# Cross-attention with layer norm on one core: small products, centring and one store moved in the last four tiles

## Chip, cores and metric

The kernel runs on one core of a Trainium2 chip. The metric is the device time in microseconds (us); lower is better. In the text PE is TensorE (matrix products), DVE is VectorE, ACT is ScalarE, POOL is GpSimd, and SP is SyncE, which in this kernel issues every transfer between HBM and the on-chip memory.

## The reference

There are 16 batches of 256 query rows of width 256, and 77 keys of width 192 for each batch. Eight heads of width 256 attend, and a layer norm over each row of 256 ends the computation:

```python
Q = (img_embed @ Wq).reshape(B, -1, H, D).transpose(0, 2, 1, 3)
K = (sent_embed @ Wk).reshape(B, -1, H, D).transpose(0, 2, 1, 3)
V = (sent_embed @ Wv).reshape(B, -1, H, D).transpose(0, 2, 1, 3)
score = jnp.einsum('bhqd,bhkd->bhqk', Q, K) / math.sqrt(D)
score = jnp.where(mask, score, -jnp.inf)
attn = jax.nn.softmax(score, axis=-1)
ctx = jnp.einsum('bhqk,bhkd->bqhd', attn, V).reshape(B, -1, H * D)
out = ctx @ Wo + img_embed
mu = jnp.mean(out, axis=-1, keepdims=True)
var = jnp.var(out, axis=-1, keepdims=True)
return (out - mu) * jax.lax.rsqrt(var + EPS) * gamma + beta
```

All data are float32. Only the last line and the sum before it concern the change.

## The kernel before

The 4096 query rows are cut into 32 tiles of 128 rows, two to a batch. A tile's rows lie on the 128 partitions; its slice of `xg` (128x256) first holds the input rows, then the sum with the attention's result, then the normalised rows, in place. Eight tiles form a group with one `xg` buffer. After a set-up stage that folds the weights together, a loop runs over the batches as a pipeline: the scores of batch b+1, the weighted sum of batch b and the layer norm of batch b-1 are issued in one turn. The order in which each engine receives its instructions is the order of the program text, written out by hand; nothing reorders it. An engine works through its own queue in that order and waits on semaphores for the others.

The last tile is number 31 (`last`). After the loop the tiles 28 to 31 are still to be finished. Each goes through these steps, whose names and lines the profile shows:

- `attend(t)`, L378: TensorE makes the attention's result `po`.
- `finish(t)`: VectorE adds `po` to the tile (L476) and takes the row statistics (L484, L487) into `mv`, the mean and the variance of each row. Tiles 28 and 29 have had this in the last turn of the loop.
- `spread(first, last)`, L495: ScalarE takes the square root of variance plus epsilon, giving `std`.
- `invert(first, last, aside)`: VectorE takes the reciprocal `rstd` (L502). For the tiles in `aside`, GpSimd then makes `less` = -mean times `rstd`, one number for each row (L506): the "small product".
- `normalise(t, aside)`. For a tile that is set aside, ScalarE computes tile times `rstd` plus `less` (L520), and GpSimd multiplies by gamma (L521) and adds beta (L522). For another tile VectorE does it in two passes: (tile - mean) times gamma (L524, which we call the centring), then times `rstd` plus beta (L527).

Tiles 29 and 30 are set aside; 28 and 31 are VectorE's. The stores go out on SP's queue: tiles 28 and 29 by one transfer of 256 KB (L535) as soon as both are done, 30 and 31 each by its own of 128 KB (L529), issued inside `normalise`. When the tail begins, GpSimd is still busy with the passes of tiles 26 and 27. The tail reads:

```python
    invert(last - 3, last - 1, aside=(last - 2,))
    normalise(last - 2, aside=True)
    finish(last - 1)
    spread(last - 1, last)
    normalise(last - 3)
    invert(last - 1, last, aside=(last - 1,))
    normalise(last - 1, aside=True)
    finish(last)
    spread(last, NT)
    invert(last, NT)
    normalise(last)
```

Of the kernel before, what the change touches and what calls it, by code (L numbers as in the profile page):

```python
# [11 lines left out]
ALU = mybir.AluOpType  # L12
# [41 lines left out]
def kernel(  # L54
# [13 lines left out]
    nc = tc.nc  # L68
# [5 lines left out]
    NG = B // GB  # L74
    QT = S // P
    NT = B * QT
    GT = GB * QT
# [50 lines left out]
    gam = const.tile([P, DI], F32, tag="gam", name="gam")  # L128
    bet = const.tile([P, DI], F32, tag="bet", name="bet")
    xg_of = {}  # L130

    x_rows = x.rearrange("b (t p) d -> p (b t) d", p=P)
    out_rows = out.rearrange("b (t p) d -> p (b t) d", p=P)
# [23 lines left out]
    xT_of, a_of, vw_of, p_of, mv_of = {}, {}, {}, {}, {}  # L157
# [215 lines left out]
    def attend(t):  # L373
        b, pT = t // QT, pT_of.pop(t)
        po = ps_mm.tile([P, DI], F32, tag="mm", name=f"po_{t}")
        for n in range(NF + 1):
            for i in range(NM):
                nc.tensor.matmul(  # L378
                    po[i * BK : (i + 1) * BK],
                    pT[:, n, i],  # L380
                    vw_of[b][:, 2 - n // 2 * 2 : 4 - n // 2 * 2, n % 2, :] if n < NF else vr[:, b, :],
                    start=(n == 0),
                    stop=(n == NF),
                )
        po_of[t] = po
# [92 lines left out]
    def finish(t):  # L478
        if t in po_of:
            add_product(t)  # L480
        g, j = t // GT, t % GT
        y = xg_of[g][:, j, :]
        bn = st.tile([P, 6], F32, tag="bn", name=f"bn_{t}")
        nc.vector.bn_stats(bn, y)  # L484
        if j == 0:
            mv_of[g] = st.tile([P, GT, 2], F32, tag="mv", name=f"mv_{g}", bufs=2)
        nc.vector.bn_aggr(mv_of[g][:, j, :], bn)  # L487
# [3 lines left out]
    def spread(first, last):  # L491

        g, lo, hi = first // GT, first % GT, (last - 1) % GT + 1
        std = st.tile([P, GT], F32, tag="std", name=f"std_{first}")
        nc.scalar.activation(std[:, lo:hi], mv_of[g][:, lo:hi, 1], AF.Sqrt, bias=eps)  # L495
        std_of[first, last] = std

    def invert(first, last, aside=()):

        g, lo, hi = first // GT, first % GT, (last - 1) % GT + 1  # L500
        rstd = st.tile([P, GT], F32, tag="rstd", name=f"rstd_{first}")
        nc.vector.reciprocal(rstd[:, lo:hi], std_of.pop((first, last))[:, lo:hi])  # L502
        if aside:
            less = st.tile([P, GT], F32, tag="less", name=f"less_{first}")
            for j in (t % GT for t in aside):
                nc.gpsimd.tensor_scalar(  # L506
                    less[:, j : j + 1], mv_of[g][:, j, 0:1], rstd[:, j : j + 1], -1.0,
                    ALU.mult, ALU.mult,
                )
        for t in range(first, last):  # L510
            j = slice(t % GT, t % GT + 1)
            rstd_of[t] = rstd[:, j], less[:, j] if aside else None

    def normalise(t, aside=False):

        g, j = t // GT, t % GT
        rstd, less = rstd_of.pop(t)
        y = xg_of[g][:, j, :]
        if aside:
            nc.scalar.activation(y, y, AF.Identity, bias=less, scale=rstd)  # L520
            nc.gpsimd.tensor_tensor(y, y, gam, ALU.mult)  # L521
            nc.gpsimd.tensor_tensor(y, y, bet, ALU.add)  # L522
        else:
            nc.vector.scalar_tensor_tensor(  # L524
                y, y, mv_of[g][:, j, 0:1], gam, ALU.subtract, ALU.mult
            )
            nc.vector.scalar_tensor_tensor(y, y, rstd, bet, ALU.mult, ALU.add)  # L527
        if t >= NT - QT:
            nc.sync.dma_start(out_rows[:, t, :], y)  # L529
            return  # L530
        done.append(t)
        if t ^ 1 in done:
            t |= 1
            j |= 1
            nc.sync.dma_start(  # L535
                out_rows[:, t + 1 - QT : t + 1, :], xg_of[g][:, j + 1 - QT : j + 1, :]
            )
# [4 lines left out]
    with tc.tile_pool(name="wonce", bufs=1) as wp:  # L542
# [23 lines left out]
        first = -(-GB * S2 // CR)  # L566
# [261 lines left out]
    last = NT - 1  # L828
    for b in range(-1, B - 1):
# [9 lines left out]
        g, n = (b + 1) // GB + 1, (b + 1) % GB  # L839
# [22 lines left out]
        if b < NS:  # L862
            if now:
                seven(b)
            nc.scalar.activation(warm, eps, AF.Exp)
            if old:
                invert(old[0], old[-1] + 1)
                normalise(old[0])
            for t in new:
                turn(t)  # L870
            if n >= NF - 2:
                for j in range((n - NF + 2) * GT // 2, (n - NF + 3) * GT // 2, 2):
                    transpose_x(g, j)
            if old:
                normalise(old[1])
            if now:
                add_seven(b)
            if b + 1 < NS:
                sums(b + 1)
            continue  # L880
        for t in now:
            attend(t)
        if b < B - 2:
            invert(old[0], old[-1] + 1, aside=old[:1])
            normalise(old[0], aside=True)
            nc.scalar.activation(warm, eps, AF.Exp)
            turn(new[0])
            normalise(old[1])
            turn(new[1])
            for t in now:  # L890
                add_product(t)
        else:
            turn(new[0])
            invert(old[0], old[-1] + 1, aside=old)
            for t in old:
                normalise(t, aside=True)
            turn(new[1])
            for t in now:
                finish(t)
            spread(now[0], now[-1] + 1)  # L900


    for t in new:
        attend(t)
    invert(last - 3, last - 1, aside=(last - 2,))
    normalise(last - 2, aside=True)
    finish(last - 1)
    spread(last - 1, last)
    normalise(last - 3)
    invert(last - 1, last, aside=(last - 1,))  # L910
    normalise(last - 1, aside=True)
    finish(last)
    spread(last, NT)
    invert(last, NT)
    normalise(last)


# [29 lines left out]
```

## Time and profile before

| what | value |
|---|---|
| median of three runs | 282.15 us (280.95, 282.15, 282.51) |
| the profiled execution, whole time | 280.93 us |
| its span (first to last instruction) | 279.2 us |
| granted TensorE clock | 0.993 |
| busy: PE, DVE, ACT, POOL | 269.7, 206.0, 166.4, 168.2 us |
| start of the last closing instructions (L942) | 278.0 to 279.1 us |
| store of 128 KB, issue to landing | 1.7 us |
| store of 256 KB, issue to landing | 2.3 us |

The span lies inside the whole time; 1.73 us lie around it. In a timeline each line gives the start in us from the span's beginning, the duration, the engine, the line of the kernel, the operation, the written and read tiles with their shapes, and in brackets how long the engine had been idle and which instruction released it. SPq is SP's queue of transfers: the time there is that of the issue, not of the transfer. The waits list adds up such idle times by engine and line.

### The profile page before, as it was taken

What the parts mean: (1) busy time and instruction counts of PE and PEld (TensorE: products, weight loads), DVE (VectorE), ACT (ScalarE), POOL (GpSimd) and SP (SyncE); (2) the same over time, 40 slices, a digit from 0 to 9 for tenths busy, and PEclk for the clock granted to TensorE, in tenths of its full rate; (3) what the DMA queues carried; (4) which work ended last, traced back from release to release, by engine and by line L of the source; (5) the groups of instructions that cost most, each with busy time, mean ns of one, the idle gap of its engine ahead of it and who ended that gap; (6) DMA issues with size and microseconds to landing.
All of it is one profiled execution on the core that took longest, in us unless ns stands there. A gap on an engine that the chain in (4) does not pass through costs nothing.

```text
span 279.2 us, 13274 instructions
## 1 busy us (share of the span) xinstructions
PE 269.7 (97%) x5924; PEld 194.8 (70%) x5924; DVE 206.0 (74%) x421; ACT 166.4 (60%) x447; POOL 168.2 (60%) x228
## 2 busy tenths in 40 slices
PE   8899999999999999999999999999999999999990
PEld 7756599976495959595959585858686858476550
DVE  0353953777738989878788888787787878788873
ACT  2303222146738586868676767777776766978751
POOL 1000069947677777787877777777778445426183
PEclk9999999999999999999999999999999999999997
DMA  6997999920000101940100009501001011010112
GB/s 198 247 223 154 305 262 236 225 82 4 2 6 2 40 5 41 190 155 4 42 2 30 16 25 190 172 5 42 4 5 40 2 42 38 4 41 2 40 39 77
DMA packets 35641, 22.61 MB, mean 81 GB/s; under 512 B 17712, under 2 KB 34048, under 8 KB 35584
## 3 DMA queue, kind: packets, MB, share of 16 engines
q1 hardware_dynamic: 35584, 21.77, 31.1%
q8 instruction: 46, 0.75, 1.2%
q14 instruction: 11, 0.09, 0.1%
HBM read 17.57 MB, written 4.19 MB: 78 GB/s over the span
## 4 chain that ended last, share of the span: by engine, by line
PE 88%; DMA 3%; POOL 2%; ACT 2%; DVE 1%; SPq 1%; issue 0%; ACTq 0%; POOLq 0%
PE ps L313 23%; PE pa L199 12%; PE pv L241 9%; PE po L429 9%; PE pm L429 7%; PE pa L213 6%; PE pv L252 5%; PE po L378 5%; DMA c_sb<-in_ctx_dram 3%; PE pu L676 3%; PE pr L274 2%; ACT e L342 1%; PE pw L690 1%; PE pgb L676 1%; PE pr L284 1%; PE pc L653 1%
## 5 line engine op out<-in xcount | busy, mean ns | idle before, releaser
L342 ACT ACTIVATE e<-s,top 128x77 f32<-128x77 f32 x256 | 67.1, 346 | 52.1 <-DVE top L335 49.9
L356 POOL TENSOR_TENSOR p<-e,rden 128x512 f32<-128x512 f32 x64 | 45.9, 739 | 46.7 <-DVE rden L350 46.4
L313 PE MATMUL ps<-a,xT 128*32 128x154 f32 x2048 | 70.0, 294 | 0.0
L313 PEld LDWEIGHTS ps<-a,xT 128*32 128x32 f32 x2048 | 66.1, 110 | 1.7 <-issue 0.8
L328 DVE TENSOR_TENSOR s<-ps,bias 128x308 f32<-128x308 f32 x64 | 30.3, 474 | 17.7 <-PE ps L313 15.9
L199 PE MATMUL pa<-cA,gA 128*32 128x308 f32 x512 | 35.8, 423 | 0.0
L462 POOL TENSOR_TENSOR xg<-xg,m 128x256 f32<-128x256 f32 x33 | 24.2, 732 | 13.5 <-DVE xg L476 11.8
L199 PEld LDWEIGHTS pa<-cA,gA 128*32 128x32 f32 x512 | 16.4, 110 | 20.9 <-issue 8.0
L241 PE MATMUL pv<-uA,cA 128*32 128x512 f32 x256 | 30.4, 592 | 0.0
L366 DVE STREAM_TRANSPOSE pT<-p 128x640 f32<-128x640 f32 x32 | 25.6, 824 | 2.4 <-POOL p L356 2.4
L348 DVE TENSOR_REDUCE den<-e 128x8 f32<-128x616 f32 x32 | 24.7, 772 | 3.4 <-ACT e L342 3.4
L335 DVE TENSOR_REDUCE top<-s 128x8 f32<-128x616 f32 x32 | 25.5, 795 | 1.1
L664 POOL COPY cB<-cB 64x224 f32<-64x224 f32 (+1 forms) x6 | 1.9, 359 | 35.2 <-DVE cB L153 35.2
L392 POOL TENSOR_TENSOR ts<-vw 128x768 f32<-128x768 f32 x11 | 21.9, 1995 | 0.0
L213 PE MATMUL pa<-cB,gB 64*32 64x308 f32 x512 | 19.5, 420 | 0.0
L378 PE MATMUL po<-vw,pT 128*32 128x256 f32 x320 | 19.2, 380 | 0.0
L859 ACT COPY vw<-pv 128x512 f32<-128x512 f32 x32 | 16.9, 579 | 2.5 <-PE pv L252 2.5
L495 ACT ACT_TABLE_LOAD x14 | 18.0, 1283 | 0.3
L213 PEld LDWEIGHTS pa<-cB,gB 64*32 64x32 f32 x512 | 9.7, 107 | 11.3 <-issue 7.6
L252 PE MATMUL pv<-uB,cB 64*32 64x512 f32 x256 | 17.4, 601 | 0.0
L524 DVE SCALAR_TENSOR_TENSOR xg<-xg,mv,gam 128x256 f32<-128x256 f32 x25 | 17.1, 683 | 0.0
L378 PEld LDWEIGHTS po<-vw,pT 128*32 128x32 f32 x320 | 10.0, 110 | 9.5 <-DVE den L348 2.5
(114 smaller groups left out, 444.9 us busy)
## 6 DMA issues: line engine op xcount, KB each, us to landing
xT<-in_x_dram SPq DMA_DIRECT2D x16, 256.0 KB, 6.2
xg<-in_x_dram SPq DMA_DIRECT2D x4, 1024.0 KB, 7.9
out_dram<-xg SPq DMA_DIRECT2D x15, 256.0 KB, 2.3
wo<-in_L_xattn_Wo_dram SPq DMA_DIRECT2D x4, 512.0 KB, 6.2
wvT<-in_L_xattn_Wv_dram SPq DMA_DIRECT2D x16, 96.0 KB, 3.0
wq_nat<-in_L_xattn_Wq_dram SPq DMA_DIRECT2D x2, 512.0 KB, 5.9
wq_blk<-in_L_xattn_Wq_dram SPq DMA_DIRECT2D x8, 128.0 KB, 5.1
wk_blk<-in_L_xattn_Wk_dram SPq DMA_DIRECT2D x8, 96.0 KB, 5.6
```

Source lines behind the costliest of these rows:

```text
L199: nc.tensor.matmul(flat(o[i * BK : (i + 1) * BK]), gA[:, h, cols(dc, i)], flat(cA[:, batches, :]), start=not B_first, stop=B_first,)
L213: nc.tensor.matmul(flat(banks[j + k][i * BK : (i + 1) * BK]), gB[half(k), h % NF, cols(dc, i)], flat(cB[half(k), batches, :]), start=B_fir ...
L241: nc.tensor.matmul(pv[k][i * BK : (i + 1) * BK], cA[:, b, k * BK : (k + 1) * BK], uA[:, parts, :, i], start=True, stop=False,)
L252: nc.tensor.matmul(pv[k][i * BK : (i + 1) * BK], cB[half(k), b, k * BK : (k + 1) * BK], uB[half(k), parts, :, i], start=False, stop=True,)
L313: nc.tensor.matmul(ps[m // 2][i * BK : (i + 1) * BK, m % 2 * 2 * S2 : (m % 2 + 1) * 2 * S2], xT_of[g][:, j * NM + m, dc], flat(a_of[g][:, ...
L328: nc.vector.tensor_tensor(s[:, a * H // 2 : (a + 1) * H // 2], ps[a][:, : H // 2 * S2].rearrange("p (h k) -> p h k", k=S2), bias[:, b, :]. ...
L335: nc.vector.tensor_reduce(top, s, AX.X, ALU.max, negate=True)
L342: nc.scalar.activation(e[:, h], s[:, h], AF.Exp, bias=top[:, h : h + 1])
L356: nc.gpsimd.tensor_tensor(part, e_mh[:, :, :, keys], rden_mh.unsqueeze(3).to_broadcast(list(part.shape)), ALU.mult,)
L366: nc.vector.transpose(pT_of[t].rearrange("p n m q -> p m n q"), p.rearrange("p m (n k) -> p m n k", k=BK),)
L378: nc.tensor.matmul(po[i * BK : (i + 1) * BK], pT[:, n, i], vw_of[b][:, 2 - n // 2 * 2 : 4 - n // 2 * 2, n % 2, :] if n < NF else vr[:, b, ...
L429: nc.tensor.matmul(out[i * BK : (i + 1) * BK], weight[:, i], moving, start=(n == 0), stop=(n == len(terms) - 1),)
```

## The change

In the tail, VectorE instead of GpSimd makes the small products of tiles 29 and 30. The first of VectorE's two passes becomes a function of its own, `centre`; for tile 28 it is issued ahead of the reciprocal of tiles 28 and 29, and for tile 31 ahead of the reciprocal of tile 31. The stores of tiles 30 and 31 leave `normalise` and are issued at the very end of the program text: that of 30 by ScalarE, behind the root of 31, and that of 31 by SP. The other uses of `invert` and `normalise` keep their instructions.

```diff
-    def invert(first, last, aside=()):
+    def invert(first, last, aside=(), less_on=nc.gpsimd):
...
-                nc.gpsimd.tensor_scalar(
+                less_on.tensor_scalar(
                     less[:, j : j + 1], mv_of[g][:, j, 0:1], rstd[:, j : j + 1], -1.0,
                     ALU.mult, ALU.mult,
                 )
...
+    def centre(t):
+        y = xg_of[t // GT][:, t % GT, :]
+        nc.vector.scalar_tensor_tensor(
+            y, y, mv_of[t // GT][:, t % GT, 0:1], gam, ALU.subtract, ALU.mult
+        )
+
+    def normalise(t, aside=False, centred=False):
...
-            nc.vector.scalar_tensor_tensor(
-                y, y, mv_of[g][:, j, 0:1], gam, ALU.subtract, ALU.mult
-            )
+            if not centred:
+                centre(t)
             nc.vector.scalar_tensor_tensor(y, y, rstd, bet, ALU.mult, ALU.add)
         if t >= NT - QT:
-            nc.sync.dma_start(out_rows[:, t, :], y)
             return
...
     for t in new:
         attend(t)
-    invert(last - 3, last - 1, aside=(last - 2,))
+    centre(last - 3)
+    invert(last - 3, last - 1, aside=(last - 2,), less_on=nc.vector)
     normalise(last - 2, aside=True)
     finish(last - 1)
     spread(last - 1, last)
-    normalise(last - 3)
-    invert(last - 1, last, aside=(last - 1,))
+    normalise(last - 3, centred=True)
+    invert(last - 1, last, aside=(last - 1,), less_on=nc.vector)
     normalise(last - 1, aside=True)
     finish(last)
     spread(last, NT)
+    centre(last)
     invert(last, NT)
-    normalise(last)
+    normalise(last, centred=True)
+    for t, queue in ((last - 1, nc.scalar), (last, nc.sync)):
+        queue.dma_start(out_rows[:, t, :], xg_of[NG - 1][:, t % GT, :])
```

More of the change, by code (lines that the diff above doesn't have):

```diff
@@ L512, in invert @@
             rstd_of[t] = rstd[:, j], less[:, j] if aside else None
-    def normalise(t, aside=False):
+    def centre(t):
[4 more added lines that the diff above has]
+    def normalise(t, aside=False, centred=False):
         g, j = t // GT, t % GT
```

## The prediction

> **What bounds the kernel now.** I read the page first: engine shares, then the chain that ended last.
>
> ```profile
> PE 269.7 (97%) x5924; PEld 194.8 (70%) x5924; DVE 206.0 (74%) x421; ACT 166.4 (60%) x447; POOL 168.2 (60%) x228
> ```
>
> TensorE carries 88% of the chain, but its last matmul (attend of tile 31) starts at 269.57 and the group ends at 271.91. All that the diff touches lies after 269.4 us, in the 9.8 us up to the span's end at 279.2. So I read the timeline of that tail, engine by engine.
>
> ```profile
> 269.25 0.18 DVE L487 BATCH_NORM_AGGREGATE mv<-bn 128x2 f32<-128x6 f32 x1
> ...
> 269.79 0.17 DVE L502 RECIPROCAL rstd<-std 128x2 f32<-128x2 f32 x1 [0.36 <-ACT std L495]
> 269.85 0.73 POOL L522 TENSOR_TENSOR xg<-xg,bet 128x256 f32<-128x256 f32 x1
> ...
> 270.56 0.27 POOL L506 TENSOR_SCALAR less<-mv,rstd 128x1 f32<-128x1 f32 x1
> ...
> 270.86 0.60 ACT L520 ACTIVATE xg<-xg,less,rstd 128x256 f32<-128x256 f32 x1 [1.10 <-POOL less L506]
> 270.88 0.45 DVE L524 SCALAR_TENSOR_TENSOR xg<-xg,mv,gam 128x256 f32<-128x256 f32 x1
> ...
> 271.36 0.49 DVE L527 SCALAR_TENSOR_TENSOR xg<-xg,rstd,bet 128x256 f32<-128x256 f32 x1
> ...
> 271.54 0.89 POOL L521 TENSOR_TENSOR xg<-xg,gam 128x256 f32<-128x256 f32 x1 [0.72 <-ACT xg L520]
> 271.77 0.16 DVE L502 RECIPROCAL rstd<-std 128x1 f32<-128x1 f32 x1
> ...
> 273.21 0.26 POOL L506 TENSOR_SCALAR less<-mv,rstd 128x1 f32<-128x1 f32 x1
> 273.51 0.60 ACT L520 ACTIVATE xg<-xg,less,rstd 128x256 f32<-128x256 f32 x1 [1.86 <-POOL less L506]
> 274.01 0.28 ACT L495 ACTIVATE std<-mv,eps 128x1 f32<-128x1 f32 x1
> 274.19 0.72 POOL L521 TENSOR_TENSOR xg<-xg,gam 128x256 f32<-128x256 f32 x1 [0.72 <-ACT xg L520]
> 274.33 0.16 DVE L502 RECIPROCAL rstd<-std 128x1 f32<-128x1 f32 x1 [1.25 <-ACT std L495]
> 274.41 0.79 DVE L524 SCALAR_TENSOR_TENSOR xg<-xg,mv,gam 128x256 f32<-128x256 f32 x1
> 274.99 0.78 POOL L522 TENSOR_TENSOR xg<-xg,bet 128x256 f32<-128x256 f32 x1
> 275.23 0.83 DVE L527 SCALAR_TENSOR_TENSOR xg<-xg,rstd,bet 128x256 f32<-128x256 f32 x1
> 275.80 0.83 SPq L529 DMA_DIRECT2D out_dram<-xg  x2
> ```
>
> Three things are to be seen. First, the bound of the tail is GpSimd's order. The reciprocal of tile 30 is ready at 271.93, but its small product waits in GpSimd's queue behind the two passes of tile 29 until 273.21: 1.3 us. ScalarE idles 1.86 us for it, and the root of tile 31, whose statistics end at 273.08, stands behind it until 274.01; VectorE idles 1.25 us for that root. Second, VectorE's two passes over tile 31 take 0.79 and 0.83 beside GpSimd, against 0.45 and 0.49 over tile 28. They end at 275.20 and 276.06, each 0.28 after the GpSimd pass beside it (274.91, 275.77). Third, the last store is issued at about 276.26 (two issues of 0.35 to 0.38 each from 275.80), though its data were ready at 276.06. The waiting at the end is the closing line of the program:
>
> ```profile
> L942 SPq EVENT_SEMAPHORE  x8: 17/28/28, 278.0 to 279.1; - x8
> ```
>
> Landing takes 1.75 us (278.0), closing another 1.2.
>
> **What the Trainium skill says.** "SBUF — State Buffer", Who interferes with whom: a VectorE operation with two SBUF inputs and a GpSimd operation that reads SBUF exclude each other for the whole instruction. The trace agrees: the ends 0.28 after GpSimd's are VectorE's bare run after a lock, and the pass at 271.54 took 0.89 instead of 0.73 when it met L527. "DMA: Bandwidth & Descriptors", Issuing engines are not separate DMA queues: issuing from a second engine saves only the sequencer's issue time. Here that is about 0.2 us, and no store of this trace was issued by ScalarE. The same SBUF section says that a VectorE tensor_scalar may enter a mode that takes the shared port too; no VectorE tensor_scalar of this size is in the trace, so it stays open below.
>
> **The change, part by part.** I write the tail out again with the same durations, lock included.
>
> *Centre of 28, ahead of the reciprocal of 28/29.* Its cover is the idle 0.36 before 269.79. It asks at 269.45, meets GpSimd's L521 until 269.77 and ends at 270.05 (+0.28), so the reciprocal slips from 269.79 to 270.07: +0.28. Behind it stand the small product, ScalarE's pass of 29 and all of tile 30. GpSimd's L522 of 27 grows by 0.05, which nothing waits for.
>
> *Small product of 29 on VectorE.* No row has it; bounds are 0.16 (reciprocal 128x1) and 0.18 (aggregate) free of the lock, or an end at GpSimd's 270.63 if it locks. I take 0.17: 270.28 to 270.45. ScalarE's pass of 29 starts at 270.49 instead of 270.86, ends at 271.09; GpSimd's passes run 271.16 to 271.89 and 271.97 to 272.75 (before 273.23).
>
> *Tile 30.* Sum and statistics (0.40 + 0.43 + 0.18 with gaps: 1.08) run 270.47 to 271.55, against 270.96 before: later by 0.6, since VectorE did more ahead of them. Root: 271.58 to 271.86. Second pass of 28 meets L521 and ends at 271.89 + 0.28 = 272.17. Reciprocal to 272.26, small product to 272.47. ScalarE's pass: 272.50 to 273.10, **1.01 earlier** than 273.51. GpSimd: 273.17 to 273.90 and 273.98 to 274.76 (before 275.77). GpSimd's two small products (0.27 + 0.26) leave its queue; the wait at 273.21 goes.
>
> *Tile 31.* The sum, ready to run at 271.98 before, now waits for VectorE until 272.47: +0.5. Statistics end at 273.57 (before 273.08), root 273.60 to 273.88, since ScalarE is free at 273.10. Centre meets L521 and ends at 273.90 + 0.28 = 274.18; the root is inside it. Reciprocal to about 274.30, last pass waits for L522 to 274.76 and ends at 275.04. Before: 276.06. **1.02 earlier.** What is late next is GpSimd's second pass of tile 30.
>
> *Stores.* Issue of 30 goes from SP to ScalarE at 274.80; behind it ScalarE has nothing. It is put behind the root of 31, so it holds up no work. SP issues 31 at 275.08 instead of 276.26: 1.18 earlier. SP keeps only the store of 28/29 before it (GpSimd's 272.75, issue 0.37, gone by 273.2). The two transfers' data took about 0.4 each in windows of 0.1 us before (276.65 to 277.1, 277.15 to 277.6), so they overlap by 0.1 at most: price 0 to 0.1. ScalarE's first use of its queue: bounded below by 0, above by the first load of SP's queue, 2.8 us to landing for 256 KB against 2.1 for stores of that size, 0.7 extra; store 30 has 0.28 in hand (274.80 + 1.75 = 276.55 against 276.83), so 0.4 shows at most. I take 0.
>
> Sum: 1.18 less 0.03 for the overlap, **1.15 us**. Span 279.2 to 278.05, the profiled execution 280.93 to 279.8. The median of the runs shown is 282.15, 1.22 above that execution; on it the sum gives 281.0, a gain of 0.41%. A measurement of this kernel tells about 0.5% (1.41 us) from no change, so the likeliest verdict is no change with a gain behind it.
>
> **The rivals.**
> 1. *The small product takes the lock.* Then each of the two ends at the end of a GpSimd pass: 29's at 270.70 (+0.25), 30's behind the L522 of 29, near 273.06 (+0.6 in all). For it: the skill's sentence. Against: one element per partition offers nothing to split. End of VectorE 275.64, last issue 275.68, gain 0.6: 281.55. Chance 0.2.
> 2. *VectorE wins its races for the port*, or the issue and closing shrink as well. If neither pass of tile 31 waits, tile 31 ends at about 274.65 and store 30 at 274.80 decides: gain up to 1.45, 280.7, just over the bound. Against: GpSimd's pass is under way at each request. Chance 0.15.
> 3. *A second queue costs more than it saves*: slower. Its place is store 30 and the ends of the program; its price, at most 0.4 shown by first use, the closing (1.2) and the 1.73 outside the span each taken twice: 3.3 in all, net 2.2 slower, 284.3. It eats the gain at 1.15 and makes the run slower by 0.5% at 2.6. For it: the trace before has no ScalarE queue. Against: one store among 15 and a first load only 0.7 slow. Chance of a net loss 0.1.
> 4. *The move does nothing*, because the port delays every VectorE pass put beside GpSimd and all slips add up: the 0.6 and 0.5 slips above already are such; another 0.5 leaves 0.6, as in 1. Counted there.
>
> **How the numbers follow.** Forecast 0.55, rivals 0.2, 0.15, 0.1. The three runs spread from 280.95 to 282.51, so a median moves by some 0.5 by itself. Faster by over 0.5% needs 1.41: a third or so of the forecast's chance (0.18) and most of the second rival's (0.12), 0.30. Slower by over 0.5%: 0.08, most of the third's, with the scatter of the others. Same: 0.62. Range: gains of 0.4 to 1.45 give 280.7 to 281.75; with 0.6 of scatter on either side, 280.1 to 282.4.
>
> **What would show it.** Right: VectorE's products near 0.17 at about 270.3 and 272.3; ScalarE's pass of 30 at 272.5 with an idle gap under 1.5; GpSimd's last pass over by 274.8; VectorE's last end 0.28 behind it; SP's last issue at 275.1, the closing at 276.9. Wrong: a product that ends with a GpSimd pass; the centre of 28 pushing the sum of 31 beyond 272.5; a store from ScalarE that lands over 2.0 us after its issue; a closing longer than 1.2. Then the last store, not the tiles, is what to look at.

## The result, and the profile after

The changed kernel takes 280.18 us (median of 7 runs, 279.54 to 280.80), the kernel before 282.15 in the same runs (280.95 to 282.90). The ratio is 0.9942, with a 95% interval of 0.9922 to 0.9963: a gain of 0.4 to 0.8%. Two more measurements of the same pair, told below, gave 0.9967 [0.9947, 0.9986] and 0.9968 [0.9952, 0.9985]. The mean of the three ratios is 0.9959. Within what a measurement of this kernel can tell, that is a gain of 0.4%, about 1.2 us.

The profiled execution went from 279.2 us of span (280.93 in all) to 278.0 (279.81 in all). The page of the changed kernel has the same shares as before; VectorE has two instructions more and GpSimd two fewer:

```profile
PE 269.4 (97%) x5924; PEld 194.2 (70%) x5924; DVE 206.6 (74%) x423; ACT 166.6 (60%) x447; POOL 167.8 (60%) x226
```

The timeline of the changed kernel's tail follows. L516 is now the centring (L524 before), L532 VectorE's last pass (L527), L526 ScalarE's pass (L520), L527 and L528 GpSimd's two (L521, L522), L924 the last stores (L529).

```profile
269.06 0.73 POOL L527 TENSOR_TENSOR xg<-xg,gam 128x256 f32<-128x256 f32 x1
...
269.26 0.18 DVE L487 BATCH_NORM_AGGREGATE mv<-bn 128x2 f32<-128x6 f32 x1
269.36 0.70 DVE L516 SCALAR_TENSOR_TENSOR xg<-xg,mv,gam 128x256 f32<-128x256 f32 x1
...
269.87 0.79 POOL L528 TENSOR_TENSOR xg<-xg,bet 128x256 f32<-128x256 f32 x1
269.99 0.15 DVE L502 RECIPROCAL rstd<-std 128x2 f32<-128x2 f32 x1
270.18 0.21 DVE L506 TENSOR_SCALAR less<-mv,rstd 128x1 f32<-128x1 f32 x1
270.31 0.41 DVE L476 TENSOR_TENSOR xg<-po,xg 128x256 f32<-128x256 f32 x1
270.43 0.60 ACT L526 ACTIVATE xg<-xg,less,rstd 128x256 f32<-128x256 f32 x1 [0.65 <-DVE less L506]
...
271.10 0.73 POOL L527 TENSOR_TENSOR xg<-xg,gam 128x256 f32<-128x256 f32 x1 [0.45 <-ACT xg L526]
...
271.32 0.80 DVE L532 SCALAR_TENSOR_TENSOR xg<-xg,rstd,bet 128x256 f32<-128x256 f32 x1
...
271.92 0.78 POOL L528 TENSOR_TENSOR xg<-xg,bet 128x256 f32<-128x256 f32 x1
272.04 0.15 DVE L502 RECIPROCAL rstd<-std 128x1 f32<-128x1 f32 x1
272.23 0.21 DVE L506 TENSOR_SCALAR less<-mv,rstd 128x1 f32<-128x1 f32 x1
272.36 0.41 DVE L476 TENSOR_TENSOR xg<-po,xg 128x256 f32<-128x256 f32 x1
272.48 0.60 ACT L526 ACTIVATE xg<-xg,less,rstd 128x256 f32<-128x256 f32 x1 [0.74 <-DVE less L506]
...
273.15 0.72 POOL L527 TENSOR_TENSOR xg<-xg,gam 128x256 f32<-128x256 f32 x1 [0.45 <-ACT xg L526]
...
273.49 0.67 DVE L516 SCALAR_TENSOR_TENSOR xg<-xg,mv,gam 128x256 f32<-128x256 f32 x1
273.55 0.29 ACT L495 ACTIVATE std<-mv,eps 128x1 f32<-128x1 f32 x1 [0.47 <-DVE mv L487]
273.95 0.78 POOL L528 TENSOR_TENSOR xg<-xg,bet 128x256 f32<-128x256 f32 x1
274.08 0.15 DVE L502 RECIPROCAL rstd<-std 128x1 f32<-128x1 f32 x1
274.26 0.75 DVE L532 SCALAR_TENSOR_TENSOR xg<-xg,rstd,bet 128x256 f32<-128x256 f32 x1
274.77 0.38 ACTq L924 DMA_DIRECT2D out_dram<-xg  x1
275.05 0.35 SPq L924 DMA_DIRECT2D out_dram<-xg  x1
```

ScalarE's pass over tile 30 starts at 272.48 instead of 273.51 and waits 0.74 us for VectorE's product instead of 1.86 for GpSimd's. VectorE's idle 1.25 us ahead of the last reciprocal is gone: the centring of tile 31 and the root run side by side from 273.5. Each of VectorE's four passes over tiles 28 and 31 ends 0.27 to 0.29 us after the GpSimd pass that it meets (270.06 after 269.79, and so on). VectorE ends tile 31 at 275.01 instead of 276.06, and SP's last issue is at 275.05 instead of 276.24. The closing line shows the shift passed on unchanged (276.9 to 278.0; it was 278.0 to 279.1):

```profile
L951 SPq EVENT_SEMAPHORE  x8: 17/28/28, 276.9 to 278.0; - x8
```

**A clock for the experiments.** Executions of one kernel differ by up to 3.0 us (280.23 to 283.23 for the kernel before, in one measurement), but not in the tail. From the first score product to the start of tile 29's aggregate (its line L487) every kernel below takes 212.64 us in its profile, within 0.01, but for the two runs with gamma and beta in PSUM (e5, e9), told below; the first score product itself begins anywhere from 56.6 to 59.0 us, after the loads. So I count from the start of tile 29's aggregate (269.25 and 269.26 above) to the last store's issue and to the span's end. This measure repeats to a few hundredths of a microsecond, where a timed ratio has an interval of 0.1 to 0.2%, 0.3 to 0.7 us, to either side:

| kernel | last issue | span's end | ratio to before, interval |
|---|---|---|---|
| before | 6.99 | 9.95 | |
| changed | 5.79 | 8.74 | 0.9942 [0.9922, 0.9963] |
| changed, second (e1) | 5.78 | 8.77 | 0.9967 [0.9947, 0.9986] |
| changed, third (e10) | 5.78 | 8.73 | 0.9968 [0.9952, 0.9985] |
| products alone (e2) | 6.93 | 9.78 | 1.0001 [0.9983, 1.0019] |
| all but the products (e3) | 6.73 | 9.47 | 0.9996 [0.9982, 1.0010] |
| both stores on SP (e4) | 5.93 | 8.86 | 0.9966 [0.9951, 0.9980] |
| changed, gamma and beta in PSUM (e5) | 5.01 | 8.02 | 0.9938 [0.9916, 0.9959] |
| the same again (e9) | 5.01 | 8.09 | 0.9939 [0.9915, 0.9963] |
| products alone, gamma and beta in PSUM (e6) | 5.87 | 8.77 | 0.9962 [0.9950, 0.9974] |
| centring of 28 not moved (e7) | 6.47 | 9.44 | 0.9981 [0.9966, 0.9997] |
| centring of 31 not moved (e8) | 6.24 | 9.06 | 0.9954 [0.9936, 0.9972] |
| product of 29 on GpSimd (e11) | 5.73 | 8.70 | 0.9949 [0.9926, 0.9972] |
| stores alone (e12) | 6.83 | 9.76 | 0.9979 [0.9963, 0.9994] |

(The last issue of before was put at 276.26 and 7.01 in the expectations; the trace has 276.24.) For every version the gain at the span's end, set against some 281.5 us, lies inside the interval of its timed ratio, for all but the products and for the stores alone only just.

### The profile page after: what moved, and what is told of

The parts are those of the page before. It is cut to its first block, busy times and chain, and to the rows that moved or that the text cites. A ratio compares the mean times of both kernels' runs of the same rounds, so it can differ in the third digit from the quotient of the medians.

```text
span 278.0 us, 13274 instructions
## 1 busy us (share of the span) xinstructions
PE 269.4 (97%) x5924; PEld 194.2 (70%) x5924; DVE 206.6 (74%) x423; ACT 166.6 (60%) x447; POOL 167.8 (60%) x226
## 4 chain that ended last, share of the span: by engine, by line
PE 89%; DVE 4%; DMA 3%; ACT 2%; SPq 1%; POOL 0%; issue 0%; POOLq 0%; ACTq 0%
PE ps L313 23%; PE pa L199 12%; PE pv L241 9%; PE po L429 9%; PE pm L429 7%; PE pa L213 6%; PE pv L252 6%; PE po L378 5%; DMA c_sb<-in_ctx_dram 3%; PE pu L680 3%; PE pr L274 2%; ACT e L342 2%; PE pw L694 1%; PE pgb L680 1%; PE pr L284 1%; PE pc L657 1%
## 5 line engine op out<-in xcount | busy, mean ns | idle before, releaser
L516 DVE SCALAR_TENSOR_TENSOR xg<-xg,mv,gam 128x256 f32<-128x256 f32 x25 | 17.2, 688 | 0.0
```

## The experiments

**Does the gain lie in the tail?** The changed kernel itself, two more times.

> The changed kernel once more, beside the others. Theory (the whole gain lies in the tail): last issue of a store at 275.05 us against 276.26 before, span shorter by 1.1 to 1.3 us, ratio 0.9955 to 0.996. Rival (something outside the tail gains too, as the medians 282.15 and 280.18 suggest): ratio below 0.9945 with the tail shorter by only 1.2.

> The changed kernel beside it: last issue at 5.78 to 5.79 us after the start of tile 29's aggregate, span from there 8.75, ratio to before between 0.9945 and 0.997.

The tail took 5.78 both times, the span's end 1.18 to 1.22 earlier than before's. The ratios, 0.9967 and 0.9968, show a little less than the 0.9955 to 0.996 expected, which lies in both intervals. The rival of a gain outside the tail falls, since the larger first gain did not come again. Of the first difference of 1.97 us between medians the tail explains 1.2. The rest is of the size of the scatter ahead of the first score product; that it arose there in those runs is not shown.

**Products alone**, on the kernel before, with the parameter `less_on` as in the change:

```diff
...
-    invert(last - 3, last - 1, aside=(last - 2,))
+    invert(last - 3, last - 1, aside=(last - 2,), less_on=nc.vector)
...
-    invert(last - 1, last, aside=(last - 1,))
+    invert(last - 1, last, aside=(last - 1,), less_on=nc.vector)
```

> The kernel before with the two small products on VectorE and nothing else. Theory (GpSimd's queue and the shared port together): ScalarE's pass of tile 29 starts at about 270.3, GpSimd's passes of 29 come 0.5 earlier and now meet both of VectorE's passes of tile 28, which end at 272.5 to 272.8 instead of 271.85; the product of 30 is made only at about 273.0, the last issue at about 276.1: gain 0.1 to 0.3 us. Rival (only the queue on GpSimd counted): product of 30 at about 272.1, last issue at about 275.3, gain 0.9 or more.

Last issue at 6.93: 0.06 us gained, where 0.1 to 0.3 was expected (0.17 at the span's end), and no timed difference. The timeline of this kernel shows both passes over tile 28 beside GpSimd's passes over 29 (L524 and L527 are VectorE's, L521 and L522 GpSimd's):

```profile
271.89 0.73 POOL L521 TENSOR_TENSOR xg<-xg,gam 128x256 f32<-128x256 f32 x1 [0.34 <-ACT xg L520]
...
272.10 0.80 DVE L524 SCALAR_TENSOR_TENSOR xg<-xg,mv,gam 128x256 f32<-128x256 f32 x1
...
272.70 0.78 POOL L522 TENSOR_TENSOR xg<-xg,bet 128x256 f32<-128x256 f32 x1
272.94 0.83 DVE L527 SCALAR_TENSOR_TENSOR xg<-xg,rstd,bet 128x256 f32<-128x256 f32 x1
...
273.88 0.21 DVE L506 TENSOR_SCALAR less<-mv,rstd 128x1 f32<-128x1 f32 x1
...
275.60 1.01 DVE L524 SCALAR_TENSOR_TENSOR xg<-xg,mv,gam 128x256 f32<-128x256 f32 x1
275.60 0.72 POOL L522 TENSOR_TENSOR xg<-xg,bet 128x256 f32<-128x256 f32 x1
```

Before, those two passes began in GpSimd's idle time and took 0.45 and 0.49, and it was GpSimd's next pass that grew (0.89). The earlier product of 29 lets GpSimd start its passes 0.6 us sooner, on top of them. They end at 273.77, and the product of 30 behind them comes 3.66 after the clock's start, against 3.96 before. Not even these 0.30 us reach the end of tile 31: its centring meets GpSimd's second pass of 30 and takes 1.01 instead of 0.79, so that VectorE ends at 6.90, later than before's 6.81. What is left of the gain at the last issue comes from SP's queue, which the store of 30 leaves sooner (issued at 6.13 instead of 6.55). The rival, which counts only GpSimd's queue, falls.

**Everything but the products**: the changed kernel with `less_on` left at GpSimd.

> The changed kernel with the two small products back on GpSimd. Theory: the product of 30 stands behind GpSimd's second pass of 29 again (about 273.2), ScalarE's pass of 30 starts at about 273.5, root of 31 at 274.1, store of 30 issued by ScalarE at about 275.8 as the last one; gain 0.4 to 0.5 us against before, 0.7 short of the change. Rival (centring and stores carry the gain, products are small change): last issue by 275.3, gain 0.9 or more.

Last issue at 6.73, by ScalarE; the span's end 0.48 earlier than before, 0.7 short of the change. The product of 30 stands again behind GpSimd's passes of 29, and there it ran into a second delay that I had not foreseen:

```profile
273.69 0.54 POOL L506 TENSOR_SCALAR less<-mv,rstd 128x1 f32<-128x1 f32 x1
273.70 0.48 DVE L516 SCALAR_TENSOR_TENSOR xg<-xg,mv,gam 128x256 f32<-128x256 f32 x1
274.27 0.60 ACT L526 ACTIVATE xg<-xg,less,rstd 128x256 f32<-128x256 f32 x1 [1.98 <-POOL less L506]
```

With VectorE's centring beside it, GpSimd's product took 0.54 instead of 0.26. The trace of the kernel before had shown the like inside the loop:

```profile
243.71 0.44 DVE L524 SCALAR_TENSOR_TENSOR xg<-xg,mv,gam 128x256 f32<-128x256 f32 x1
243.79 0.48 POOL L506 TENSOR_SCALAR less<-mv,rstd 128x1 f32<-128x1 f32 x1
```

The timed ratio, 0.9996, shows no gain. By the profiles neither half is worth much alone: 0.17 us at the span's end for the products, 0.48 for the rest, 1.21 together.

**Is it the shared port?** The changed kernel, with the operand moved that the two engines meet on. Gamma, beta and the tiles lie in SBUF, the main on-chip memory; PSUM is the other one, which holds TensorE's results such as `po`. ScalarE copies gamma and beta into a PSUM bank; VectorE's passes over 28 and 31 read them there.

```diff
+    on_dve = {"gam": gam, "bet": bet}
...
-            y, y, mv_of[t // GT][:, t % GT, 0:1], gam, ALU.subtract, ALU.mult
+            y, y, mv_of[t // GT][:, t % GT, 0:1], on_dve["gam"], ALU.subtract, ALU.mult
...
-            nc.vector.scalar_tensor_tensor(y, y, rstd, bet, ALU.mult, ALU.add)
+            nc.vector.scalar_tensor_tensor(y, y, rstd, on_dve["bet"], ALU.mult, ALU.add)
...
                 normalise(t, aside=True)
+            gb = ps_mm.tile([P, 2, DI], F32, tag="mm", name="gb")
+            nc.scalar.copy(gb[:, 0], gam)
+            nc.scalar.copy(gb[:, 1], bet)
+            on_dve["gam"], on_dve["bet"] = gb[:, 0], gb[:, 1]
             turn(new[1])
```

> The changed kernel with gamma and beta copied by ScalarE into a PSUM bank (two copies in its idle time after the passes of tiles 26 and 27), and VectorE's four passes over tiles 28 and 31 reading them there, so that each has one operand in SBUF instead of two. Times are counted from the start of tile 29's aggregate (last issue of a store: 7.01 us before, 5.79 changed). Theory (VectorE's passes are long because of a port shared with GpSimd): each pass takes 0.45 to 0.55 instead of 0.67 to 0.80, wherever GpSimd runs; GpSimd's second passes fall from 0.78 to 0.73; VectorE ends tile 31 at about 4.9 to 5.0, ScalarE issues the store of 30 at about 5.05 as the last: 0.7 us more than the change gains, ratio to before about 0.993. Rival (the passes are long for another reason, the place in the tail or a busy SBUF): durations stay, last issue at 5.8.

```profile
270.46 0.73 POOL L528 TENSOR_TENSOR xg<-xg,gam 128x256 f32<-128x256 f32 x1
...
270.77 0.45 DVE L517 SCALAR_TENSOR_TENSOR xg<-xg,mv,gb 128x256 f32<-128x256 f32 x1
...
272.35 0.73 POOL L528 TENSOR_TENSOR xg<-xg,gam 128x256 f32<-128x256 f32 x1 [0.34 <-ACT xg L527]
...
272.56 0.45 DVE L533 SCALAR_TENSOR_TENSOR xg<-xg,rstd,gb 128x256 f32<-128x256 f32 x1
...
274.54 0.48 DVE L517 SCALAR_TENSOR_TENSOR xg<-xg,mv,gb 128x256 f32<-128x256 f32 x1
274.93 0.72 POOL L529 TENSOR_TENSOR xg<-xg,bet 128x256 f32<-128x256 f32 x1
...
275.13 0.48 DVE L533 SCALAR_TENSOR_TENSOR xg<-xg,rstd,gb 128x256 f32<-128x256 f32 x1
275.64 0.35 SPq L929 DMA_DIRECT2D out_dram<-xg  x1
275.69 0.38 ACTq L929 DMA_DIRECT2D out_dram<-xg  x1
```

All four passes take 0.45 to 0.48 in the same company, GpSimd's second pass of 30 falls from 0.78 to 0.72, and the last issue is at 5.01, where about 5.05 was expected. The port theory stands; the rival of a busy place falls. The changed kernel's own timeline agrees: its sums (L476), which take `po` from PSUM, last 0.41 us with GpSimd's passes beside them (270.31, 272.36). This version is better in the tail than both kernels. It ran a second time beside the changed kernel:

> The version with gamma and beta in PSUM for VectorE once more, on one chip with the changed kernel. Theory: last issue 5.01 us after the start of tile 29's aggregate as in its first run, and 0.7 to 0.8 us less time than the changed kernel's in the same call. Rival (the tail's gain is lost to the two copies or elsewhere): no difference between the two medians.

The tail was the same, 5.01. The medians, 280.11 against 280.42, lie 0.3 us apart, where 0.7 to 0.8 were expected; the ratios to before, 0.9939 and 0.9968, lie 0.8 us apart, but their intervals overlap. So the timed runs alone neither separate the two versions nor rule out the rival. The profiles show a part of the gain lost: in this version the stretch from the first score product to tile 29's aggregate takes 212.88 and 212.79 us instead of 212.64, longer in one step, at the scores of tiles 18 and 19. The next kernel has the same two copies and lacks that step, so the copies alone do not bring it; what does stays open.

**Products alone, with the port out of the way**: the edit of products alone and the one with PSUM, both on the kernel before.

> The kernel before with the small products on VectorE (as in the run with that alone, last issue at 6.93 us after the start of tile 29's aggregate, nothing gained) and gamma and beta in PSUM for VectorE's passes; no centring moved, both stores on SP. Theory (the products alone gained nothing only because GpSimd's earlier passes of 29 lock out VectorE's passes over 28): the two passes over 28 take about 1.0 together instead of 1.6, the product of 30 is made at about 3.0 instead of 3.7, last issue at about 5.8: as good as the whole change. Rival (the products are of no use without the centring moved into the waits): last issue at 6.5 or later.

Last issue at 5.87: what gained 0.06 us now gains 1.12, with no centring moved. The rival falls.

```profile
271.40 0.73 POOL L522 TENSOR_TENSOR xg<-xg,gam 128x256 f32<-128x256 f32 x1 [0.33 <-ACT xg L521]
...
271.61 0.45 DVE L525 SCALAR_TENSOR_TENSOR xg<-xg,mv,gb 128x256 f32<-128x256 f32 x1
...
272.10 0.48 DVE L528 SCALAR_TENSOR_TENSOR xg<-xg,rstd,gb 128x256 f32<-128x256 f32 x1
...
272.69 0.21 DVE L507 TENSOR_SCALAR less<-mv,rstd 128x1 f32<-128x1 f32 x1
```

The passes over 28 run free beside GpSimd's, and the product of 30 comes 2.96 after the clock's start instead of 3.66: 0.70 of the 1.06 us that this version wins over the products alone. The rest is won at tile 31, whose centring takes 0.46 instead of 1.01. These collisions, over 28 and again over 31, were what made the products worthless alone.

**Centring of 28 not moved:**

```diff
-    centre(last - 3)
     invert(last - 3, last - 1, aside=(last - 2,), less_on=nc.vector)
...
-    normalise(last - 3, centred=True)
+    normalise(last - 3)
```

> The changed kernel with both passes over tile 28 behind the statistics of 30, as before; the centre of 31 stays ahead of its reciprocal. Theory: as in the run with products alone up to the product of 30 (3.7 us after the start of tile 29's aggregate), then the centre of 31 beside GpSimd's first pass of 30; last issue at about 6.45, 0.5 to 0.6 short of before's 7.01 and 0.65 behind the change. Rival (the centre of 28 costs its 0.28 of delay and wins nothing): last issue at 5.5.

Last issue at 6.47. The passes over 28 took 0.80 and 0.83 and ended at 3.55 after the clock's start, 0.7 later than in the changed kernel; the product of 30 followed. The centring costs 0.2 us of delay where it stands (reciprocal at 269.99 instead of 269.79) and is worth 0.68 by the last issue.

**Centring of 31 not moved:**

```diff
-    centre(last)
     invert(last, NT)
-    normalise(last, centred=True)
+    normalise(last)
```

> The changed kernel with the first pass over tile 31 behind its reciprocal again. Theory: up to the statistics of 31 nothing changes; then the centre starts at about 4.7 us after the start of tile 29's aggregate, together with GpSimd's second pass of 30, is locked out by it and ends 0.28 after it at about 5.75, the last pass runs free (0.48); last issue at about 6.3, 0.5 behind the change. Rival (the root's wait is too short for the centre to win anything, since GpSimd's second pass of 30 sets the end): last issue within 0.1 of 5.79.

```profile
274.12 1.00 DVE L516 SCALAR_TENSOR_TENSOR xg<-xg,mv,gam 128x256 f32<-128x256 f32 x1
274.13 0.72 POOL L528 TENSOR_TENSOR xg<-xg,bet 128x256 f32<-128x256 f32 x1
...
275.17 0.48 DVE L532 SCALAR_TENSOR_TENSOR xg<-xg,rstd,bet 128x256 f32<-128x256 f32 x1
```

The two records begin within 0.01 us of one another, GpSimd runs its bare 0.72, and VectorE ends 0.27 after it: last issue at 6.24, 0.45 behind the change. The rival, that GpSimd's second pass sets the end, falls. The timed ratio does not show the 0.45 us; it is within its interval.

**Which product?** The changed kernel with `less_on` removed from the line of tile 29 alone.

> The changed kernel with the small product of tile 29 alone back on GpSimd; that of 30 stays on VectorE. Theory (only the product of 30 was on the path; 29's passes merely have to be over when 30's begin): 29's passes come 0.5 later, VectorE's second pass over 28 then runs free (0.45 instead of 0.80), the product of 30 is made at about 2.7 to 2.9 us after the start of tile 29's aggregate, last issue at 5.8 to 5.9 against 5.79: within 0.1 us of the change. Rival (both products are needed): last issue at 6.3 or later.

Last issue at 5.73, no worse than the change. The product of 29 comes later, but VectorE's second pass over 28 then ran free (0.46). Only the product of tile 30 carries; moving that of 29, a part of the change, was not needed.

**The stores.** First the changed kernel with `(last - 1, nc.sync)` in place of `nc.scalar`, then the kernel before with only the stores moved.

> The changed kernel with both last stores issued by SP, 30 and then 31. Theory (a second queue saves its issue time only): store of 30 at 274.77, store of 31 at 275.2 instead of 275.05, span 0.1 to 0.2 us longer than the change's, time around the span 1.7 to 1.8 as before. Rival (a second queue costs or saves something at the start, the closing or around the span): span or the time around it differs from the change's by more than 0.3 us.

> The kernel before with only the two last stores moved to the end of the text, 30 on ScalarE and 31 on SP. Theory (only the issue time is saved): store of 30 at about 6.55 us after the start of tile 29's aggregate as before, store of 31 at about 6.85 instead of 7.01; gain 0.1 to 0.2 us, ratio 0.999 to 1. Rival (a second queue matters by itself): span or time around it off by over 0.3 us.

With both on SP the last issue moved from 5.79 to 5.93 and the end by 0.1. The stores alone brought 0.16 at the issue and 0.19 at the end. The time around the span lay between 1.73 and 1.86 us in every run of these two kernels, of the changed kernel and of before. A second queue saves its issue time and no more, as the expectation had it. The timed ratio of the stores alone, 0.9979 [0.9963, 0.9994], puts the gain at 0.17 us or more, where 0.999 to 1 was expected; the profile's 0.19 lies at that edge.

## Why the prediction was right, point by point

**The bound** was read correctly: GpSimd's order held up the product of 30, and the root of 31 behind it. In the kernel before the product, at 273.21, followed directly on GpSimd's second pass of 29:

```profile
272.51 0.72 POOL L522 TENSOR_TENSOR xg<-xg,bet 128x256 f32<-128x256 f32 x1
```

The change moved ScalarE's pass by 1.03 us (1.01 predicted). The product's move alone brings 0.36 of it (3.90 after the clock's start instead of 4.26), since VectorE's passes over 28 then stand in the way. The prediction had the collision of the second of these passes in its sum, but did not say what each part is worth without the others; the experiments do.

**The sum.** Predicted 1.15 us; the span's end moved by 1.21 on the common clock. (With the 276.24 of the trace for the last issue before, the sum would have been 1.13.) The three ratios average 0.41%, the very figure forecast; with 0.2% to either side of each, so close a match is luck. Step by step:

| step | predicted | measured |
|---|---|---|
| centring of 28 ends | 270.05 | 270.06 |
| reciprocal of 28/29 starts | 270.07 | 269.99 |
| product of one tile | 0.17 | 0.21 |
| sum of 30 starts | 270.47 | 270.31 |
| second pass of 28 ends | 272.17 | 272.12 |
| ScalarE's pass of 30 starts | 272.50 | 272.48 |
| centring of 31 ends | 274.18 | 274.16 |
| VectorE ends tile 31 | 275.04 | 275.01 |
| store of 31 issued | 275.08 | 275.05 |
| span | 278.05 | 278.0 |

The product was sized too small, but VectorE starts an independent instruction some 0.08 before the one ahead of it is over, so the sum of 30 came earlier all the same. The port then wiped out the difference: a pass that waits for GpSimd ends 0.27 to 0.29 after GpSimd's, whenever it was issued.

**The price of the lock** was right as a number and wrong as a reading. The prediction took 0.28 us from the trace and called it VectorE's bare run after a lock; the bare run is 0.45 to 0.49. So a pass that waited takes some 0.2 us less after GpSimd's end than it takes alone. Why stays open.

**Where the numbers were off.** The overlap of the two stores' data was charged at 0.03 and didn't show. The median of 280.18 is 0.8 below the 281.0 forecast and lies just inside the range of 280.1 to 282.4. The first ratio is 0.58%, where a gain of less than 0.5% was held the likeliest; its interval reaches to 0.37%, and the repeats, at 0.33 and 0.32%, are below 0.5%. The fault is not in the sum but in the base: 282.15 was the median of three runs, and of the seven of the first measurement, but the later measurements, with 57, 41 and 38 runs of the kernel before, gave 281.26, 281.70 and 281.53. The changed kernel's medians were 280.18, 280.41 and 280.42. The 0.5% that a measurement was said to tell from no change was too coarse: none of the three intervals contains 1. And the trace has 17 stores, 15 of 256 KB and two of 128, not 15.

**The rivals.** The product does not take the port: 0.21 us with GpSimd's pass running throughout (270.18 beside the pass from 269.87 to 270.66), and 0.21 with GpSimd idle (273.88, products alone). VectorE won no race in the tail of 31. The second queue cost nothing: ScalarE's store landed 1.7 us after its issue, and the closing took 1.1. The slips did not add up beyond the sum.

## What to carry to other kernels

When an engine is relieved, look at what its earlier start will run into: here moving the small products gained next to nothing until the passes they set free no longer fell on VectorE's. A VectorE pass with two SBUF operands that waits for GpSimd is to be priced by GpSimd's end plus a tail taken from the trace (0.28 us here, less than the bare run), or freed of the port by putting one operand in PSUM. For edits at the end of a long kernel, count from a late event that all versions share; a microsecond is clear there that the scatter of the loads hides in the whole time.

## What the runs showed of the hardware that I had not expected

- One number per partition is enough to wait for the port: GpSimd's product took 0.54 us beside a VectorE pass with two SBUF operands, and 0.48 in the loop of the kernel before, against 0.26 alone. VectorE's own product, which has no second tensor operand, took 0.21 beside GpSimd and alone.
- Which engine goes first when both begin together followed no plain rule. With the centring of 31 not moved, and with the products alone, the two records begin within 0.01 us and GpSimd went first (VectorE's pass 1.00 and 1.01 instead of 0.45). With all but the products, 273.69 and 273.70 are as close, and VectorE went first (0.48; GpSimd's product 0.54). In the first two cases VectorE's record begins while its reciprocal is still running, so it may have asked later than its start says.
- A VectorE pass with one operand in PSUM was no slower than with both in SBUF and GpSimd idle: 0.45 to 0.48 against 0.45 to 0.49.
